# A two-way linear scan: own terms moved to identity and diagonal products in PSUM, and group statistics from an accumulator

## The chip, the cores and the metric

The kernel runs on one core of a Trainium2 chip. The metric is the device time of one execution in microseconds. Engines are named as in the profile: PE (matmuls), PEld (weight loads of the same engine), DVE (vector), ACT (scalar, activation functions), POOL and SP (here mostly the queue that issues DMAs).

## The reference

A network of four residual layers on `x` of shape 32 x 192 x 56 x 56 in fp32. Each layer normalises its input over 32 groups of 6 channels and adds its output to `x`. The layers are an agent attention (L0), a two-way RWKV scan (L1), a shift by learned offsets with a 3x3 filter (L2) and a long convolution with a 55x55 filter (L3). Only L1 is touched by the change. What matters of it (shortened, with the running maximum of the reference left out, which only guards against overflow):

```python
k, v, r = xs @ Wk.T, xs @ Wv.T, xs @ Wr.T          # xs: pixels x channels
def wkv(w, u, k, v):                               # per channel, along the pixels
    p = q = 0
    for t in pixels:
        y[t] = (p + exp(u + k[t]) * v[t]) / (q + exp(u + k[t]))
        p = exp(w) * p + exp(k[t]) * v[t]
        q = exp(w) * q + exp(k[t])
x_bi = 0.5 * (wkv(forwards) + wkv(backwards))
h = sigmoid(r) * x_bi
h = layernorm_over_channels(h) * ln_g + ln_b
x = x + h @ Wo.T
```

The term with `exp(u + k[t])` is called the own term here: a pixel's own contribution, weighted by `exp(u)`, that is added to what the recurrence carried up to the pixel before. The output `x` of this layer is called x2. The next layer needs its mean and variance per image and group of six channels.

## The kernel before, in words

The kernel has stages one after the other: the filter of L3 and the attention L0, then the scans of L1 (`scan_pairs`), then L2 and L3 together. `scan_pairs` works on pairs of images. A pair's 2 x 192 channels make three tiles of 128 partitions: the first 128 channels of either image, and the last 64 of both together. The 3136 pixels are cut into NM = 4 strips of MC = 784, and a matmul takes half a strip, 392 columns, since a PSUM bank holds 512 fp32 values. `turned()` hands out a PSUM tile of two banks, four of which rotate and fill PSUM. `_Pairs.outer` multiplies the first two tiles by a 192 x 192 weight, in parts called `aa` and `ca`, `_Pairs.inner` the third, in parts called `cc` and `ac`.

For one pair and strip there are four functions:

- `forwards` normalises x (ACT), multiplies by `wk` and `wv` (PE), takes `ek = exp(k)` (ACT) and `bv = ek * v` (DVE), and runs the forward scan.
- `backwards` multiplies the same normalised x by `wr`, makes the sigmoid `g` on ACT, and runs the backward scan over the stored `ek` and `bv`, from the last strip to the first. Then it forms `h = (y_f + y_b) * g` on DVE.
- `finish` centres `h` over the channels (`centre`, PE), squares it (ACT), averages the squares (`mean_w`, PE), multiplies `h` by `wog` (PE), scales by the inverse deviation (`rd`), adds the bias and x (L1170), takes `bn_stats` of the result for the next layer's group statistics (`stats_of`, L986), and stores x2.
- `measure` loads strips of a pair further on and takes `bn_stats` of them, for the first normalisation.

The main loop takes, for every pair and strip, `backwards` of this pair, `finish` of the strip before, `forwards` of the next pair, and in two of four steps two calls of `measure` for the pair after that. `deviations`, `norm` and `conclude` turn statistics into scales. `grouped` does small matmuls with one column for them. PE takes its instructions in the program's order. The order on DVE and ACT is made by a scheduler when the program is built.

The function `scan` is called once for each pair, strip, tile and direction. It handles two recurrences, `p` over `bv` and `q` over `ek`. DVE runs the recurrence with `tensor_tensor_scan` (L1070), writing it one column to the side, so that each pixel's place holds the state before it. POOL copies the carried state into the edge column and out of the last (L1065, L1071). Then DVE adds the own term by one `scalar_tensor_tensor` (L1072) on the whole strip:

```python
nc.vector.tensor_tensor_scan(out, decay[:, of(t)].to_broadcast([128, MC]), data, at, ALU.mult, ALU.add)
nc.gpsimd.tensor_copy(at, z[:, last : last + 1])
nc.vector.scalar_tensor_tensor(before, src, c, before, ALU.mult, ALU.add)
```

where `src` is `bv` or `ek` and `c` is `exp(u)`, one value per partition. `inverse` takes 1/q on ACT as a logarithm and an exponential (L1077, L1078), and DVE multiplies the two (L1113 forwards, L1134 backwards).

Of the kernel before, what the change touches and what calls it, by code (L numbers as in the profile page):

```python
# [876 lines left out]
def scan_pairs(ctx: ExitStack, tc: tile.TileContext, a, k, x1, x2, rs2, wogT, count):  # L877
# [15 lines left out]
    def small(name, shape):  # L893
        return cp.tile(shape, F32, name=name, tag=name)
# [6 lines left out]
        return [t[:, h * HM : (h + 1) * HM] for h in range(2)]  # L901


    wo = [small("wo_a", [128, C]), small("wo_c", [64, C])]
    lg = [small("lg_a", [128, 1]), small("lg_c", [64, 1])]
    lb = [small("lb_a", [128, 1]), small("lb_c", [64, 1])]
    cen = [small("cen_a", [128, C]), small("cen_c", [64, C])]
    for i, r in enumerate((slice(0, 128), slice(128, C))):
        nc.sync.dma_start(out=wo[i], in_=a["L1_conv_WoT"][r])
        nc.sync.dma_start(out=lg[i], in_=a["L1_conv_ln_g"][r].unsqueeze(1))  # L910
# [10 lines left out]
    for i, r in enumerate((slice(0, 128), slice(128, C))):  # L921
        n = (128, 64)[i]
        ps, _, _ = turned()
        for s in range(2):
            nc.tensor.matmul(ps[:n, 0, :C], cen[s][:, r], wo[s], start=(s == 0), stop=(s == 1))
        turn = wp.tile([128, C], F32, name="turn", tag="turn", bufs=1)
        nc.vector.tensor_copy(turn[:n], ps[:n, 0, :C])
        nc.sync.dma_start(out=wogT[r], in_=turn[:n])

    wk, wv, wr = (blocks(n, a[f"L1_conv_{n}T"]) for n in ("Wk", "Wv", "Wr"))  # L930
    wog, centre, mean_w, group = (
# [2 lines left out]
    wd = pairs.vector("wd", a["L1_conv_w_decay"])  # L934
    eu = pairs.vector("eu", a["L1_conv_u"])
    nc.scalar.activation(eu, eu, AF.Exp)

    w = small("w", [128, 2])
    nc.scalar.activation(w, wd, AF.Exp)
# [64 lines left out]
        pairs.inner(group, [ps[:, 1, 2:3]], [[s] for s in src])  # L1004
        return ps[:, :, 1], ps[:, 1, 2:3]

    def deviations(st):

        mv = moments(st)
        first, third = grouped([mv[:, t, 0:1] for t in range(3)])  # L1010
        mean = sp.tile([128, 3], F32, name="mean", tag="mean", bufs=4)
        nc.vector.tensor_copy(mean[:, 0:2], first)
        nc.vector.tensor_copy(mean[:, 2:3], third)
        d = sp.tile([128, 3], F32, name="d", tag="d", bufs=4)
        nc.vector.tensor_tensor(d, mv[:, :, 0], mean, ALU.subtract)
        nc.vector.tensor_tensor(d, d, d, ALU.mult)
        nc.vector.tensor_tensor(d, d, mv[:, :, 1], ALU.add)
        return mean, d
# [20 lines left out]
    class State:  # L1039


        def __init__(self, p, scaling):
            self.p, (_, self.rs, self.nb) = p, scaling
            self.seen = sp.tile([128, 5, 3 * NM], F32, name="seen", tag="seen", bufs=3)
            self.ek, self.bv, self.y = {}, {}, {}
            self.fore, self.back = start("f"), start("b")
            self.st2 = new_stats("st2")

    def normed(s, m):
        xs = load(s.p, m)  # L1050
# [1 line left out]
            nc.scalar.activation(xs[t], xs[t], AF.Identity, bias=s.nb[:, t : t + 1], scale=s.rs[:, t : t + 1])  # L1052
        return [parts(t) for t in xs]

    def scan(s, m, t, carry, rev):

        b, e = s.bv[m][t], s.ek[m][t]
        c = eu[:, of(t)]
        got = []
        for i, src in enumerate((b, e)):  # L1060
            z = wp.tile([128, MC + 1], F32, name="pq"[i], tag="pq", bufs=5)
            edge, last = (MC, 0) if rev else (0, MC)
            out, before = (z[:, 0:MC], z[:, 1:]) if rev else (z[:, 1:], z[:, 0:MC])
            at = carry[t][i]
            nc.gpsimd.tensor_copy(z[:, edge : edge + 1], at)  # L1065
            if rev:
                out, data = out[:, ::-1], src[:, ::-1]
            else:
                data = src[:, :]
            nc.vector.tensor_tensor_scan(out, decay[:, of(t)].to_broadcast([128, MC]), data, at, ALU.mult, ALU.add)  # L1070
            nc.gpsimd.tensor_copy(at, z[:, last : last + 1])  # L1071
            nc.vector.scalar_tensor_tensor(before, src, c, before, ALU.mult, ALU.add)  # L1072
            got.append(before)
        return got

    def inverse(s, den, m, t, which):
        nc.scalar.activation(den, den, AF.Ln)  # L1077
        nc.scalar.activation(den, den, AF.Exp, scale=-1.0, accum_out=s.seen[:, which, 3 * m + t : 3 * m + t + 1])  # L1078

    def start(way):  # L1080
        carry = [[sp.tile([128, 1], F32, name=f"{way}{i}{t}", tag=f"{way}{i}{t}") for i in range(2)] for t in range(3)]
# [5 lines left out]
    def forwards(s, m):  # L1087
        s.ek[m] = [kp.tile([128, MC], F32, name="ek", tag="ek") for _ in range(3)]
        s.bv[m] = [kp.tile([128, MC], F32, name="bv", tag="bv") for _ in range(3)]
        s.y[m] = [kp.tile([128, MC], F32, name="y", tag="y", bufs=3 * NM + 4) for _ in range(3)]  # L1090
        xn = normed(s, m)
        for tiles in ((0, 1), (2,)):
            for wt in (wk, wv):
                ps = [turned() for _ in tiles]
                if len(tiles) == 2:
                    pairs.outer(wt, [q[2] for q in ps], xn)
                else:
                    pairs.inner(wt, ps[0][2], xn)
                for t, (_, both, _) in zip(tiles, ps):
                    if wt is wk:  # L1100
                        nc.scalar.activation(
                            s.ek[m][t].rearrange("p (h n) -> p h n", h=2), both, AF.Exp,
                            accum_out=s.seen[:, 0, 3 * m + t : 3 * m + t + 1],
                        )
                    else:
                        nc.vector.tensor_tensor(
                            s.bv[m][t].rearrange("p (h n) -> p h n", h=2), both,
                            s.ek[m][t].rearrange("p (h n) -> p h n", h=2), ALU.mult,
                        )
            for t in tiles:  # L1110
                num, den = scan(s, m, t, s.fore, False)
                inverse(s, den, m, t, 1)
                nc.vector.tensor_tensor(s.y[m][t], num, den, ALU.mult)  # L1113

    def backwards(s, m):
        xn = normed(s, m)
        h = s.y[m]
        for tiles in ((0, 1), (2,)):
            ps = [turned() for _ in tiles]
            if len(tiles) == 2:  # L1120
                pairs.outer(wr, [q[2] for q in ps], xn)
            else:
                pairs.inner(wr, ps[0][2], xn)
            for t, (_, both, _) in zip(tiles, ps):
                g = wp.tile([128, MC], F32, name="g", tag="t")
                nc.scalar.activation(
                    g.rearrange("p (h n) -> p h n", h=2), both, AF.Exp, scale=-1.0,
                    accum_out=s.seen[:, 3, 3 * m + t : 3 * m + t + 1],
                )
                nc.scalar.activation(g, g, AF.Ln, bias=1.0)  # L1130
                nc.scalar.activation(g, g, AF.Exp, scale=-1.0)
                num, den = scan(s, m, t, s.back, True)
                inverse(s, den, m, t, 2)
                nc.vector.tensor_tensor(num, num, den, ALU.mult)  # L1134
                nc.vector.tensor_tensor(h[t], h[t], num, ALU.add)
                nc.vector.tensor_tensor(h[t], h[t], g, ALU.mult)

    def finish(s, m):
# [20 lines left out]
        for tiles in ((0, 1), (2,)):  # L1159
            po = [turned() for _ in tiles]  # L1160
            if len(tiles) == 2:
                pairs.outer(wog, [q[2] for q in po], hs)
            else:
                pairs.inner(wog, po[0][2], hs)
            for t, (_, out, _) in zip(tiles, po):
                rd = rds[t]
                rdh = rd.rearrange("p (h n) -> p h n", h=2)
                nc.scalar.activation(rd, rd, AF.Exp, scale=-0.5)
                nc.vector.tensor_tensor(rdh, out, rdh, ALU.mult)
                nc.vector.scalar_tensor_tensor(xs[t], rd, cb[:, of(t)], xs[t], ALU.add, ALU.add)  # L1170
                stats_of(s.st2, m, t, xs[t])
        rows = slice(m * MC // S, (m + 1) * MC // S)
        for r, t, i, c in places:
            nc.sync.dma_start(out=x2[c, i, rows, s.p], in_=xs[t][r].rearrange("p (h w) -> p h w", w=S))
# [20 lines left out]
        for t, x in enumerate(load(p, m)):  # L1195
            stats_of(st, m, t, x)

    s, after, before = State(0, norm(*deviations(stats_for(0)))), norm(*deviations(stats_for(1))), None
    for m in range(NM):
        forwards(s, m)  # L1200
    for p in range(last):
        ahead = State(p + 1, after) if p + 1 < last else None
        st = new_stats("st1")
        for i in range(NM):
            m = NM - 1 - i
            backwards(s, m)
            if i > 0:
                finish(s, m + 1)
            elif before is not None:
                finish(before, 0)  # L1210
            if ahead is not None:
                forwards(ahead, i)
            if p + 2 < last:
                if i < 2:
                    measure(st, p + 2, 2 * i)
                    measure(st, p + 2, 2 * i + 1)
                elif i == 2:
                    spread = deviations(st)
                else:
                    after = norm(*spread)  # L1220
            if before is not None:
                if i == 1:
                    before.spread = deviations(before.st2)
                elif i == 2:
                    conclude(before)
        before, s = s, ahead
    finish(before, 0)
    before.spread = deviations(before.st2)
    conclude(before)
    nc.sync.dma_start(out=rs2[0:128], in_=kept_a)  # L1230
    for i, r in enumerate((slice(0, 64), slice(64, 128))):
# [580 lines left out]
```

## Time and profile before

| | us |
|---|---|
| runs | 12775.48, 12757.16, 12770.67 |
| median | 12770.67 |
| profiled execution, its time | 12763.6 |
| profiled execution, its span | 12761.8 |

Of the span, the attention and all ahead of it take 0 to 4997 us, the set-up of the scans 4997 to 5081, the scans 5081 to 8816, the end of their statistics 8816 to 8830, and the two last layers the rest. The busy time of the engines over the span is PE 11522.3 us, PEld 7190.8, DVE 11221.3, ACT 5979.7 and POOL 2199.4.

The profile comes from one execution. Its slices show the busy share of each engine in tenths, PEclk the clock that was granted to PE. A row of a group gives the line, the engine, the operation, what it writes and reads, how often, then busy time in us and the mean of one in ns, and behind the last bar the idle time of that engine just before it, with what ended it. In the timeline the columns are start (us), duration (us), engine, line, operation and how many records are merged. An fp32 matmul of the code leaves two records on PE, and the records of following matmuls overlap.

### The profile page before, as it was taken

Reading aid. Unit: us, or ns where it says so; the run is one execution under the profiler, and the core shown is the slowest. Engines: PE = TensorE matmul, PEld = TensorE weight load, DVE = VectorE, ACT = ScalarE, POOL = GpSimd, SP = SyncE. Lnnn points to the kernel's source line nnn. Section 1 sums busy time; section 2 is a strip of 40 time slices with the busy share of each in tenths; the row PEclk is TensorE's granted clock in tenths of the full one; section 3 lists DMA queues with packets and bytes.
Section 4 is the critical chain, followed back from the end, with each engine's and each line's share of the span. In section 5 each row is a group of like instructions: output and inputs, shape, how many; then the busy total and the mean of one; then the engine's idle time right before and its main releaser. Section 6 shows DMA issues by size and latency. Waiting matters only on the chain. (4 is left out here: it accounts for less than half of the span.)

```text
span 12761.8 us, 165194 instructions
## 1 busy us (share of the span) xinstructions
PE 11522.3 (90%) x63158; PEld 7190.8 (56%) x63158; DVE 11221.3 (88%) x15929; ACT 5979.7 (47%) x11146; POOL 2199.4 (17%) x2238
## 2 busy tenths in 40 slices
PE   4999999999999997788878788787999999999999
PEld 1556555565555564333333333334777777777777
DVE  3888888888888886999999999998888888888888
ACT  2554554554554553555555555554333333333333
POOL 0000000000000000544445454544000000000000
PEclk8999999999999998889988899898999999999999
DMA  2111111111111112344443344433111111111111
GB/s 64 40 39 39 39 39 49 47 39 39 39 41 53 41 39 68 84 110 103 99 110 97 105 107 103 103 98 81 43 42 44 42 44 44 42 42 44 43 44 28
DMA packets 949574, 770.40 MB, mean 60 GB/s; under 512 B 769870, under 2 KB 811065, under 8 KB 939760
## 3 DMA queue, kind: packets, MB, share of 16 engines
q1 hardware_dynamic: 948776, 759.74, 22.7%
q8 instruction: 504, 8.26, 0.3%
q14 instruction: 294, 2.41, 0.1%
HBM read 479.96 MB, written 240.50 MB: 56 GB/s over the span
## 5 line engine op out<-in xcount | busy, mean ns | idle before, releaser
L589 DVE SCALAR_TENSOR_TENSOR o<-v_a,dww,o 128x896 f32<-128x896 f32 (+1 forms) x1024 | 1053.0, 1028 | 396.5 <-ACT v_a L563 314.2
L1739 ACT COPY y<-ps 64x252 f32<-64x252 f32 (+1 forms) x2376 | 806.4, 339 | 1132.6 <-PE ps L1733 1102.1
L1657 PE MATMUL ps<-f,real 84*84 84x112 f32 x6144 | 1090.8, 259 | 0.0
L1657 PE MATMUL ps<-f,imag 84*84 84x112 f32 x6144 | 1089.4, 259 | 0.0
L1664 ACT COPY z<-ps 84x448 f32<-84x448 f32 x768 | 405.0, 527 | 1219.9 <-PE ps L1657 1218.4
L1657 PEld LDWEIGHTS ps<-f,real 84*84 84x84 f32 x6144 | 783.9, 153 | 134.3 <-issue 95.8
L1084 POOL MEMSET f<- 128x1 f32 x96 | 8.8, 98 | 4810.6 <-PE ps L739 4805.6
L1077 ACT ACTIVATE q<-q 128x784 f32<-128x784 f32 x384 | 328.9, 857 | 999.1 <-DVE q L1072 753.0
L1657 PEld LDWEIGHTS ps<-f,imag 84*84 84x84 f32 x6144 | 763.8, 153 | 0.0
L606 ACT ACTIVATE pr<-ps,low 98x896 f32<-98x896 f32 (+1 forms) x384 | 351.9, 916 | 838.0 <-DVE low L604 838.0
L602 PE MATMUL ps<-xs_a,gk_a 128*98 128x448 f32 (+1 forms) x1536 | 637.8, 496 | 0.0
L589 DVE SCALAR_TENSOR_TENSOR o<-v_c,dww,o 128x448 f32<-128x448 f32 (+1 forms) x1024 | 634.1, 619 | 4.0
L603 PE MATMUL ps<-xs_c,gk_c 125*98 125x448 f32 (+1 forms) x1536 | 631.9, 492 | 0.0
L694 PE MATMUL ps<-gq_a,xs_a 128*112 128x294 f32 x1792 | 606.2, 419 | 19.2 <-DVE pq L699 19.2
L1674 PE MATMUL ps<-z,f 84*114 84x448 f32 x1536 | 608.9, 539 | 0.0
L695 PE MATMUL ps<-gq_c,xs_c 125*112 125x294 f32 x1792 | 596.4, 414 | 0.0
L1523 POOL TENSOR_TENSOR mat<-tap,tap 114x114 f32<-114x114 f32 x96 | 40.6, 423 | 3163.0 <-PE ps L1583 2310.0
L1631 PE MATMUL re<-y,f 128*84 128x420 f32 (+1 forms) x1152 | 532.0, 542 | 8.7 <-ACT y L1739 7.3
L1631 PE MATMUL im<-y,f 128*84 128x420 f32 (+1 forms) x1152 | 526.8, 538 | 0.0
L1733 PEld LDWEIGHTS ps<-f,padded 114*128 114x128 f32 x3168 | 471.5, 191 | 96.5 <-issue 70.4
L1733 PE MATMUL ps<-f,padded 114*128 114x168 f32 x3168 | 501.9, 310 | 21.4 <-DVE o L1676 10.0
L707 ACT ACTIVATE pq<-pq 112x1176 f32<-112x1176 f32 x224 | 265.3, 1184 | 525.1 <-DVE pq L699 401.9
(358 smaller groups left out, 29470.4 us busy)
## 6 DMA issues: line engine op xcount, KB each, us to landing
x<-x SPq DMA_DIRECT2D x640, 392.0 KB
x<-x SPq DMA_DIRECT2D x640, 196.0 KB
x<-x SPq DMA_DIRECT2D x192, 399.0 KB
out_x<-x SPq DMA_DIRECT2D x384, 196.0 KB
x_a<-in_x SPq DMA_DIRECT2D x32, 1568.0 KB
x<-x_a SPq DMA_DIRECT2D x32, 1568.0 KB
x_c<-in_x SPq DMA_DIRECT2D x64, 392.0 KB
x<-x_c SPq DMA_DIRECT2D x64, 392.0 KB
```

Of the source, the lines that this page charges most:

```text
L589: nc.vector.scalar_tensor_tensor(dst, tap(i), dww[:, t, i : i + 1], dst, ALU.mult, ALU.add)
L602: mm(ps[P2, h, :n], g[:, cols], xs_a[j][:, px], start=True, stop=False)
L603: mm(ps[P2, h, :n], gk_c[0:KC, 2 * j + h, cols], xs_c[j][0:KC, px], start=False, stop=True)
L606: nc.scalar.activation(pr[:, :, :n], ps[P2, :, :n], AF.Exp, bias=low[:, j, p : p + 1], accum_out=sums[:, j, p : p + 1])
L694: mm(ps[:SUB, i, :HA], xs_a[j][:, px], g, start=True, stop=False)
L695: mm(ps[:SUB, i, :HA], xs_c[j][0:KC, px], gq_c[0:KC, 2 * j + (q + i) // ns], start=False, stop=True)
L1631: nc.tensor.matmul(ps[:, : n * 84], f2[:, i, :], y[:, i0 : i0 + n].rearrange("p g s u -> p (g s u)"), start=True, stop=True)
L1657: nc.tensor.matmul(ps[:84, i * 2 * S : (i + 1) * 2 * S], part[:, i0 + i].rearrange("p s u -> p (s u)"), f3[:, m, :], start=(m == 0), stop= ...
L1664: nc.scalar.copy(z[:, i0 : i0 + n].rearrange("p g m w -> p (g m w)"), ps[:84, : n * 2 * S])
L1674: nc.tensor.matmul(got, f4[:, m, :], z[:, i0 : i0 + n, m, :], start=(m == 0), stop=(m == 1))
L1733: nc.tensor.matmul(ps[:, g * 168 : (g + 1) * 168], flat[:, (g0 + g) * 128 : (g0 + g + 1) * 128], f1, start=True, stop=True)
L1739: nc.scalar.copy(y[64 * m : 64 * m + 64, 2 * g0 + i : 2 * (g0 + n) : 2], got[64 * i : 64 * i + 64, :, :, m, :])
```

## The change

The own terms leave DVE. Two diagonal matrices `own[0]`, `own[1]` hold `exp(u)`, and `ident` is the identity, loaded by one more DMA at the set-up. For each recurrence of a scan, PE multiplies `src` by `own` and the shifted recurrence by `ident`, both into the same PSUM tile, for each half of the strip. The denominator `q` now goes first. ACT takes its logarithm from PSUM and writes the result into a tile of SBUF (`y` forwards, a new `den` backwards). The numerator stays in PSUM, where the final product on DVE reads it.

The statistics of x2 change too. The residual step (L1170 before) gives out the sum of its result by its accumulator. ACT squares the result about a near value, the negative mean of the last strip (which is the first that `finish` takes of a pair), and accumulates the squares. The two `bn_stats` per tile and strip of x2 are gone. `moments_of` makes mean and variance of the sums; the `bn_stats` of `measure` stay. A few constants of the set-up move into working tiles.

```diff
+    ident = small("ident", [128, 128])
+    nc.sync.dma_start(out=ident, in_=k["ident"])
+    own = [small(f"own{i}", [128, 128]) for i in range(2)]
+    for i in range(2):
+        nc.vector.tensor_scalar(own[i], ident, eu[:, i : i + 1], None, ALU.mult)
...
+    def moments_of(s):
+
+        mv = sp.tile([128, 3, 2], F32, name="mv2", tag="mv2")
+        nc.vector.tensor_reduce(mv[:, :, 0], s.sums, AX.X, ALU.add)
+        nc.vector.tensor_reduce(mv[:, :, 1], s.squares, AX.X, ALU.add)
+        nc.vector.tensor_scalar(mv, mv, 1.0 / N, None, ALU.mult)
+        nc.vector.tensor_tensor(s.away, s.away, mv[:, :, 0], ALU.add)
+        nc.vector.tensor_tensor(s.away, s.away, s.away, ALU.mult)
+        nc.vector.tensor_tensor(mv[:, :, 1], mv[:, :, 1], s.away, ALU.subtract)
+        nc.vector.tensor_scalar(mv[:, :, 1], mv[:, :, 1], 0.0, None, ALU.max)
+        return mv
...
-    def scan(s, m, t, carry, rev):
+    def scan(s, m, t, carry, rev, den, which):
 
-        b, e = s.bv[m][t], s.ek[m][t]
-        c = eu[:, of(t)]
-        got = []
-        for i, src in enumerate((b, e)):
+        for i, src in ((1, s.ek[m][t]), (0, s.bv[m][t])):
...
             nc.vector.tensor_tensor_scan(out, decay[:, of(t)].to_broadcast([128, MC]), data, at, ALU.mult, ALU.add)
             nc.gpsimd.tensor_copy(at, z[:, last : last + 1])
-            nc.vector.scalar_tensor_tensor(before, src, c, before, ALU.mult, ALU.add)
-            got.append(before)
-        return got
-
-    def inverse(s, den, m, t, which):
-        nc.scalar.activation(den, den, AF.Ln)
-        nc.scalar.activation(den, den, AF.Exp, scale=-1.0, accum_out=s.seen[:, which, 3 * m + t : 3 * m + t + 1])
+            _, both, halves = turned()
+            for w, rhs, first in ((own[of(t).start], src, True), (ident, before, False)):
+                for half, part in zip(halves, parts(rhs)):
+                    nc.tensor.matmul(half, w, part, start=first, stop=not first)
+            if i == 1:
+                nc.scalar.activation(den.rearrange("p (h n) -> p h n", h=2), both, AF.Ln)
+                nc.scalar.activation(
+                    den, den, AF.Exp, scale=-1.0, accum_out=s.seen[:, which, 3 * m + t : 3 * m + t + 1]
+                )
+        return both
...
             for t in tiles:
-                num, den = scan(s, m, t, s.fore, False)
-                inverse(s, den, m, t, 1)
-                nc.vector.tensor_tensor(s.y[m][t], num, den, ALU.mult)
+                y = s.y[m][t]
+                num = scan(s, m, t, s.fore, False, y, 1)
+                y = y.rearrange("p (h n) -> p h n", h=2)
+                nc.vector.tensor_tensor(y, num, y, ALU.mult)
...
-                num, den = scan(s, m, t, s.back, True)
-                inverse(s, den, m, t, 2)
-                nc.vector.tensor_tensor(num, num, den, ALU.mult)
-                nc.vector.tensor_tensor(h[t], h[t], num, ALU.add)
+                den = wp.tile([128, MC], F32, name="den", tag="t")
+                num = scan(s, m, t, s.back, True, den, 2)
+                both = den.rearrange("p (h n) -> p h n", h=2)
+                nc.vector.tensor_tensor(both, num, both, ALU.mult)
+                nc.vector.tensor_tensor(h[t], h[t], den, ALU.add)
...
-                nc.vector.scalar_tensor_tensor(xs[t], rd, cb[:, of(t)], xs[t], ALU.add, ALU.add)
-                stats_of(s.st2, m, t, xs[t])
+                nc.vector.scalar_tensor_tensor(
+                    xs[t], rd, cb[:, of(t)], xs[t], ALU.add, ALU.add, accum_out=s.sums[:, t, m : m + 1]
+                )
+                if m == NM - 1:
+                    nc.vector.tensor_scalar(
+                        s.away[:, t : t + 1], s.sums[:, t, m : m + 1], -1.0 / MC, None, ALU.mult
+                    )
+                nc.scalar.activation(
+                    rd, xs[t], AF.Square, bias=s.away[:, t : t + 1], accum_out=s.squares[:, t, m : m + 1]
+                )
```

More of the change, by code (lines that the diff above doesn't have):

```diff
@@ L901, in parts, with passing @@
         return [t[:, h * HM : (h + 1) * HM] for h in range(2)]
-    wo = [small("wo_a", [128, C]), small("wo_c", [64, C])]
+    def passing(n):
+        return wp.tile([128, MC], F32, name="passing", tag="t")[:n, :C]
+    wo = [passing(128), passing(64)]
     lg = [small("lg_a", [128, 1]), small("lg_c", [64, 1])]
     lb = [small("lb_a", [128, 1]), small("lb_c", [64, 1])]
-    cen = [small("cen_a", [128, C]), small("cen_c", [64, C])]
+    cen = [passing(128), passing(64)]
     for i, r in enumerate((slice(0, 128), slice(128, C))):
@@ L925, in scan_pairs @@
             nc.tensor.matmul(ps[:n, 0, :C], cen[s][:, r], wo[s], start=(s == 0), stop=(s == 1))
-        turn = wp.tile([128, C], F32, name="turn", tag="turn", bufs=1)
-        nc.vector.tensor_copy(turn[:n], ps[:n, 0, :C])
-        nc.sync.dma_start(out=wogT[r], in_=turn[:n])
+        turn = passing(n)
+        nc.vector.tensor_copy(turn, ps[:n, 0, :C])
+        nc.sync.dma_start(out=wogT[r], in_=turn)
     wk, wv, wr = (blocks(n, a[f"L1_conv_{n}T"]) for n in ("Wk", "Wv", "Wr"))
@@ L1005, in grouped, with deviations @@
         return ps[:, :, 1], ps[:, 1, 2:3]
-    def deviations(st):
-        mv = moments(st)
+    def moments_of(s):
[8 more added lines that the diff above has]
+        return mv
+    def deviations(mv):
         first, third = grouped([mv[:, t, 0:1] for t in range(3)])
@@ L1046, in __init__ @@
             self.fore, self.back = start("f"), start("b")
-            self.st2 = new_stats("st2")
+            self.sums, self.squares = (sp.tile([128, 3, NM], F32, name=n, tag=n, bufs=3) for n in ("sums", "squares"))
+            self.away = sp.tile([128, 3], F32, name="away", tag="away", bufs=3)
     def normed(s, m):
@@ L1196, in measure @@
             stats_of(st, m, t, x)
-    s, after, before = State(0, norm(*deviations(stats_for(0)))), norm(*deviations(stats_for(1))), None
+    s, after, before = State(0, norm(*deviations(moments(stats_for(0))))), norm(*deviations(moments(stats_for(1)))), None
     for m in range(NM):
@@ L1217, in scan_pairs @@
                 elif i == 2:
-                    spread = deviations(st)
+                    spread = deviations(moments(st))
                 else:
@@ L1222, in scan_pairs @@
                 if i == 1:
-                    before.spread = deviations(before.st2)
+                    before.spread = deviations(moments_of(before))
                 elif i == 2:
@@ L1227, in scan_pairs @@
     finish(before, 0)
-    before.spread = deviations(before.st2)
+    before.spread = deviations(moments_of(before))
     conclude(before)
```

## The prediction

> **What bounds the kernel now.** First the page's slices of the span, 319 us each.
>
> ```profile
> PE   4999999999999997788878788787999999999999
> PEld 1556555565555564333333333334777777777777
> DVE  3888888888888886999999999998888888888888
> ACT  2554554554554553555555555554333333333333
> ...
> PEclk8999999999999998889988899898999999999999
> ```
>
> Slices 16 to 27 are the scan stage, the only one whose code changes. There DVE is at 9 and PE, elsewhere at 9, is at 7 or 8 with a lower granted clock. So DVE is full and PE has gaps. How large the gaps are is the question, and next comes the table by stretches. The scan stage runs from the first `Wk` matmul (5081) to the last `wog` matmul (8816). The second row is a stretch of the later stages, where PE is the full engine.
>
> ```profile
> core 0: us, PE busy (x) PEld busy (x) DVE busy (x) ACT busy (x) POOL busy (x), PEclk, DMA share, GB/s
> 5081.00:8816.00 3735.00, 3031.46 (x10800) 1385.79 (x10802) 3656.97 (x4059) 2163.80 (x3578) 1862.21 (x1699) 0.90 0.40 101
> 9100.00:12700.00 3600.00, 3557.20 (x24277) 2742.15 (x24276) 3119.30 (x5241) 1289.90 (x3109) 262.84 (x395) 1.00 0.17 42
> ```
>
> DVE is busy for 3657 of 3735 us (98%): it sets this stage. PE is busy for 3031 us at a mean clock of 0.90. Without gaps it had 1.00, so its work at full clock is about 3031 x 0.90 = 2728 us, and 3735 - 2728 = 1007 us is what PE could still take. Next, the groups of that stretch on DVE, for what goes away.
>
> ```profile
> L1072 DVE SCALAR_TENSOR_TENSOR q<-ek,eu,q 128x784 f32<-128x784 f32 x384 | 391.8, 1024 | 0.5
> L1072 DVE SCALAR_TENSOR_TENSOR p<-bv,eu,p 128x784 f32<-128x784 f32 x384 | 386.5, 1020 | 0.0
> L986 DVE BATCH_NORM_STATS2 st<-x 128x6 f32<-128x392 f32 x714 | 361.6, 554 | 6.2 <-DMA x<-x 6.2
> ```
>
> Last, PE's timeline where it runs without gaps at full clock, for the price of what is added.
>
> ```profile
> 6553.32 1.58 PE L870 MATMUL ps<-x,Wk_cc 128*128 128x392 f32 x4
> 6554.84 1.54 PE L873 MATMUL ps<-x,Wk_ac 128*64 128x392 f32 x8
> 6556.30 1.58 PE L870 MATMUL ps<-x,Wv_cc 128*128 128x392 f32 x4
> 6557.82 1.54 PE L873 MATMUL ps<-x,Wv_ac 128*64 128x392 f32 x8
> 6559.28 0.38 PE L1002 MATMUL ps<-d,grp_aa 128*128 128x1 f32 x2
> ...
> 6561.05 2.90 PE L860 MATMUL ps<-x,Wr_aa 128*128 128x392 f32 x8
> ...
> 6570.37 2.90 PE L860 MATMUL ps<-y,cen_aa 128*128 128x392 f32 x8
> 6573.20 1.59 PE L863 MATMUL ps<-y,cen_ca 64*128 64x392 f32 x8
> 6574.72 1.58 PE L870 MATMUL ps<-y,cen_cc 128*128 128x392 f32 x4
> 6576.23 1.54 PE L873 MATMUL ps<-y,cen_ac 128*64 128x392 f32 x8
> ```
>
> The column to read is the start, not the duration: matmuls overlap in the records, so a group costs the distance to the next group's start. Each matmul of the code leaves two records (both `cc` matmuls of a group are "x4"). Two full 128x128 matmuls on 392 columns with one weight (`cc`) cost 1.51 to 1.52 us, four (`aa`) 2.83, four half-height ones (`ca`) 1.52, four half-width ones (`ac`) 1.46. So a further record costs about 0.33 us ((2.83 - 1.515) / 4), and a change of weight about 0.2 us on top (1.515 - 4 x 0.33).
>
> **The sum for PE.** There are 16 pairs x 4 strips = 64 steps. A step has five weights at 2.83 + 1.52 + 1.51 + 1.46 = 7.32 us (`wk`, `wv`, `wr`, `centre`, `wog`) and `mean` at 2.83 + 1.52 = 4.35: 40.95 us, 2621 us for 64. The small group sums (58 at 6561.05 - 6559.28 = 1.77 us) add 103: 2724 us, which agrees with the 2728 above. The change adds, per scan, `own` on `ek`, `ident` on `q`, `own` on `bv`, `ident` on `p`, two full matmuls each: four `cc`-like groups of 1.515 us, 6.06 us. With 64 x 3 tiles x 2 directions = 384 scans that is 384 x 6.06 = 2327 us. PE then has 2724 + 2327 = 5051 us to do in a stage that takes 3735. It has 1007 us of room and gets 2327.
>
> The Trainium skill, "TensorE: Matmul & The Clock Gate", section "Back-to-back issue gap", gives N/2.4 + 2.5 ns for a warm matmul, 166 ns for 392 columns; by that the addition would be an estimated 510 us and fit. The rows above say 0.66 us for the two records, and they decide. The skill's "Perfetto Trace Analysis", section "Identifying the Most-Contended Engine", would judge TensorE's headroom by weight loads rather than matmul time; by PEld's 1386 of 3735 us (37%) PE would be far from full here, and DVE's saving would be the gain. The start-to-start distances contradict that for 392-column fp32 matmuls.
>
> **DVE.** Removed: 768 multiply-adds (L1072) at 1.02 us by the rows, 786 us, and the 384 `bn_stats` of x2 (L986) at 0.55, 213 us. Records of DVE overlap a little, so the gain is nearer 900 than 999 us. Added: seven small operations instead of three `bn_aggr` per pair, 48 copies of -sum/784, `own`: a few us. The accumulator on the residual step (L1170) is not in the trace on DVE; ScalarE's read of its accumulator takes 0.19 us, so 0 to 0.19 x 192 = 36 us. The final products now read PSUM; L1169, which does so, takes 0.96 us like L1113, which does not: nothing. DVE falls to about 2770 us.
>
> **ACT.** 192 squares like L1149's (0.81 + 0.19 us) add 193 us, and the logarithm of the denominators reads PSUM (L1126's 0.81 instead of L1077's 0.86), -18. ACT goes from 2164 to about 2340 us, far from full. POOL's 128x1 copies stay; the products on `ident` now wait for the one that fills the edge column, as L1077 did.
>
> **What becomes late.** PE runs in the program's order, while DVE's order is a scheduled one: in the changed kernel as built DVE does both tiles' scans (`q`, `q`, `bv`, `bv`, `p`, `p`) before the first final product. So while PE spends 6.06 us on a scan's products, DVE needs 2 x 1.84 + 0.96 = 4.6 us for it, and the next `ident` finds its scan done. What can stop PE is a strip of `x`. In two of four steps the strips that are measured for a later pair share the seven `x` buffers, and their `bn_stats` stand on DVE ahead of the `rd` products that free PSUM for `wk` and `wv`. Before, PE lost 176 + 80 us waiting for a normalised `x` (L860, L863 on ACT L1052) by the waits of PE, the nearest rows there are. The bounds are 0 and 256; I take 150, since the DVE queue that made some of these waits is now short. The set-up's one more DMA and two small products are a few us at most.
>
> Stage: 5051 + 150 = 5201 us, against 3735: +1466. The profiled execution took 12763.6 us, so 14230; the median of the runs is 7 us above it, so 14237, say **14240 us**. The cover for DVE's saving is gone the other way round: DVE's 900 us fall into time in which PE is the last to finish.
>
> **Rivals.**
> *Cheaper changes of weight.* If the load of `ident` or `own` hides behind the running matmuls, 1536 groups lose 0.2 us, 307 us: 13930. Against it, every `cc` row shows the gap, with 128-column weights of the same size.
> *PE waits for each scan.* If DVE held a tile's scan behind the previous tile's final product, `ident` would come 0.96 + 1.84 - 1.515 = 1.3 us late, 384 times: 499 us, 14740. DVE's scheduled order speaks against it, PE's fixed order and four PSUM tiles for it.
> *Not slower.* The new products cost one record each, not two, or overlap in pairs as `ca` does. Break-even is (3735 - 2724) / 3072 = 0.33 us per matmul, one record. Below it DVE's 2770 us and PE share the stage; at half of that PE has 2724 + 507 + 150 = 3381 and the time is about 12410. Against it: these are full 128x128 fp32 matmuls like `cc`, which never shows under 0.66.
> *The change half works.* If the squares or the PSUM readers held up ACT, the time would still be PE's, as ACT has 2860 us to spare.
>
> **How the numbers follow.** Forecast 0.80; cheaper weights 0.07; waiting for scans 0.10; not slower 0.03, of which most is faster. The range goes from 13960, near the cheaper weights, to 14560, which takes the whole 256 us of strip waits and part of the wait for scans. A difference of 0.2% (25 us) is what the runs can tell from none: faster 0.02, same 0.01, slower 0.97.
>
> **What would show it.** After: PE near 97% busy through the stage at a granted clock of 1.00, DVE near 53%, `own` and `ident` groups 1.51 us apart, PE the stage's chain. The lines of L1072 and half of L986 are gone. It is wrong if DVE is still at 95% or more, if the new groups stand well under 1.3 us apart, or if PE shows idle time in front of `ident`, released by scans, of more than 300 us in sum.

## The result, and the profile after

| | before | after |
|---|---|---|
| median of the runs, us | 12771.16 (12757.16 to 12775.48) | 13877.79 (13871.16 to 13887.6) |
| profiled execution, time and span | 12763.6, 12761.8 | 13871.16, 13869.4 |
| scan stage, first `Wk` to last `wog` | 5081 to 8816: 3735 | 5069.7 to 9920.7: 4851 |
| DVE busy in the stage | 3657 | 2895 |
| PE busy in the stage, granted clock | 3031 at 0.90 | 4794 at 0.99 |

The change makes the kernel slower: the ratio is 1.0869, with an interval of 1.085 to 1.0888. The forecast said 14240 with a range from 13960. The direction and the engine were right, and the time fell below the range.

The slices of the page after, now 347 us each; slices 14 to 28 are the scan stage.

```profile
PE   4999999999999979999999999999899999999999
PEld 2656556556556545555555555555577777777777
DVE  4888888888888866565656656565588888888888
ACT  2455455554554534545454544545433333333333
...
PEclk8999999999999989999999999999999999999999
```

PE and DVE have changed places. Between the two end slices, which also hold other stages, PE is at 9 with its full clock, and DVE is at 5 or 6. The table by stretches gives the numbers.

```profile
core 0: us, PE busy (x) PEld busy (x) DVE busy (x) ACT busy (x) POOL busy (x), PEclk, DMA share, GB/s
5069.70:9920.70 4851.00, 4793.75 (x16942) 2457.73 (x16940) 2894.52 (x3211) 2419.67 (x3956) 669.74 (x1699) 0.99 0.32 78
```

PE is busy for 99% of the stage and DVE for 60%. On DVE the multiply-adds of the own terms are gone; of `bn_stats` the strips of `measure` are left, and the accumulator is read 190 times at 0.081 us (groups of the stage on DVE):

```profile
L995 DVE BATCH_NORM_STATS2 st<-x 128x6 f32<-128x392 f32 x336 | 176.4, 560 | 369.4 <-DMA x<-x 368.6
L1194 DVE DVE_READ_ACCUMULATOR x<-rd,cb,x 128x1 f32 x190 | 15.4, 81 | 0.0
```

What counts is the price of the new groups. This is PE's timeline from the forward scans of tiles 0 and 1 to the third tile. Again the column to read is the start.

```profile
7048.38 1.59 PE L863 MATMUL ps<-x,Wv_ca 64*128 64x392 f32 x8
7049.90 1.58 PE L1094 MATMUL ps<-ek,own 128*128 128x392 f32 x4
7051.32 1.48 PE L1094 MATMUL ps<-q,ident 128*128 128x392 f32 x4
7053.09 1.55 PE L1094 MATMUL ps<-bv,own 128*128 128x392 f32 x4 [0.29 <-DVE bv L1128]
7055.73 1.56 PE L1094 MATMUL ps<-p,ident 128*128 128x392 f32 x4 [1.08 <-DVE p L1089]
7057.12 1.48 PE L1094 MATMUL ps<-ek,own 128*128 128x392 f32 x4
7058.44 1.48 PE L1094 MATMUL ps<-q,ident 128*128 128x392 f32 x4
7059.75 1.48 PE L1094 MATMUL ps<-bv,own 128*128 128x392 f32 x4
7061.07 1.48 PE L1094 MATMUL ps<-p,ident 128*128 128x392 f32 x4
7062.39 1.48 PE L870 MATMUL ps<-x,Wk_cc 128*128 128x392 f32 x4
7063.80 1.54 PE L873 MATMUL ps<-x,Wk_ac 128*64 128x392 f32 x8
7065.27 1.58 PE L870 MATMUL ps<-x,Wv_cc 128*128 128x392 f32 x4
7066.78 1.54 PE L873 MATMUL ps<-x,Wv_ac 128*64 128x392 f32 x8
7068.25 1.59 PE L1094 MATMUL ps<-ek,own 128*128 128x392 f32 x4
```

From 7057.12 to 7062.39 four groups, each with another weight than the one before, stand 1.317 us apart. That is four records of 0.329 us and nothing for the change of weight. The same `cc` form costs 1.41 us where a full group stands ahead and a half-width one behind (`Wk_cc`, 7062.39 to 7063.80), and 1.51 where half-width groups stand on both sides (`Wv_cc`, 7065.27 to 7066.78). So what the forecast took for a change of weight goes with the change of *form*: about 0.1 us in a full group's distance at each border to half tiles. In the kernel before, a full group had half tiles ahead of it, behind it or on both sides; of the 1536 new groups 256 have such a border and the others none.

The waits of PE in the stage:

```profile
PE ps L1094 <- DVE p L1089: 31.3, 29, 1.1
PE ps L1094 <- DVE bv L1128: 23.9, 27, 1.1
```

These are waits for the first tile's numerator in some of the steps, as at 7053 and 7055 above. The waits for a strip of `x` that the forecast had put at 150 us are gone.

### The profile page after: what moved, and what is told of

It reads as the page before. It is cut to its first block, busy times and chain, and to the rows that moved or that the text cites. A ratio compares the mean times of both kernels' runs of the same rounds, so it can differ in the third digit from the quotient of the medians.

```text
span 13869.4 us, 177711 instructions
## 1 busy us (share of the span) xinstructions
PE 13277.6 (96%) x69302; PEld 8267.0 (60%) x69302; DVE 10454.9 (75%) x15083; ACT 6239.0 (45%) x11530; POOL 1006.9 (7%) x2238
## 5 line engine op out<-in xcount | busy, mean ns | idle before, releaser
L1094 PE MATMUL ps<-p,ident 128*128 128x392 f32 x1536 | 571.0, 494 | 31.3 <-DVE p L1089 31.3
L1094 PE MATMUL ps<-ek,own 128*128 128x392 f32 x1536 | 594.9, 510 | 0.2 <-ACT ek L1123 0.2
L1094 PE MATMUL ps<-bv,own 128*128 128x392 f32 x1536 | 570.0, 494 | 23.9 <-DVE bv L1128 23.9
L1089 DVE TENSOR_TENSOR_SCAN p<-decay,b,bv 128x784 f32<-128x784 f32 x192 | 353.8, 1843 | 316.3 <-PE ps L1094 310.1
L1094 PE MATMUL ps<-q,ident 128*128 128x392 f32 x1536 | 569.5, 493 | 1.5 <-DVE q L1089 1.3
L1074 ACT ACTIVATE x<-x,nb,rs 128x784 f32<-128x784 f32 x384 | 396.1, 1033 | 318.2 <-DMA x<-x 196.4
```

The lines of the kernel that those rows point to most:

```text
L1094: nc.tensor.matmul(half, w, part, start=first, stop=not first)
```

## The experiments

The medians of the kernel before in these runs were 12762.1 us (e1 to e4), 12768.72 (e5 to e8) and 12769.82 (e9 to e12).

### What a change of weight costs (e1)

Matmuls alone on data at rest, in sections, with everything else taken out. It computes nothing of the reference and ran once. Three of its sections (shortened, `mm` is the matmul):

```python
    # 2 two weights in turn, on top
    for i in range(G):
        for h in range(2):
            mm(p[i // 2 % 2][h], (wa, wb)[i % 2], (s, o)[i % 2][h], start=i % 2 == 0, stop=i % 2 == 1)
    # 3 two weights in turn, each product another weight
    for i in range(2 * G):
        mm(p[0][0] if i % 2 else p[1][0], (wa, wb)[i % 2], s[0], start=True, stop=True)
...
    # 5 full, then four of half width in another tile of PSUM
    for i in range(G // 2):
        for h in range(2):
            mm(p[i % 2][h], wa, s[h], start=True, stop=True)
        for h in range(2):
            for r in (low, high):
                mm(p[2 + i % 2][h][r], wn, o[h], start=True, stop=True)
```

> A kernel of matmuls alone (it computes nothing of the reference; the output is x with four numbers of the products in it). All products are fp32 on 392 columns, in seven stretches behind one of warming up: one full 128x128 weight; the same, each pair on top of the pair before in PSUM; two full weights in turn, pair by pair; two in turn, product by product; a full pair and four half-width products on top of it, as cc and ac; the same with the half-width products in another PSUM tile; four full and four half-height ones, as aa and ca; half-width ones alone. Theory (what costs is the change between full and half tiles, about 0.1 us or a little more each way; a change of weight between full tiles is hidden): full pairs 1.32 us apart in all stretches with full tiles alone, also when the weight changes with every product (0.66 us each); full pair plus half-width four 2.98 us, whether on top or in another PSUM tile; four full plus four half-height 4.35 us; half-width fours alone 1.32. Rival of the prediction (a change of weight costs 0.2 us): pairs with two weights in turn 1.515, product by product 0.86. Second rival (adding on top of what was just written costs): 1.32 for one weight on fresh tiles, more for one weight on top, and 2.63 for the half-width products in another tile.

Its timeline, one stretch from each of three sections:

```profile
134.11 1.48 PE L49 MATMUL p<-src,wa 128*128 128x392 f32 x4
135.43 1.48 PE L49 MATMUL p<-other,wb 128*128 128x392 f32 x4
...
258.54 0.82 PE L52 MATMUL p<-src,wb 128*128 128x392 f32 x2
259.20 0.82 PE L52 MATMUL p<-src,wa 128*128 128x392 f32 x2
...
334.95 1.58 PE L63 MATMUL p<-src,wa 128*128 128x392 f32 x4
336.46 1.54 PE L66 MATMUL p<-other,wn 128*64 128x392 f32 x8
```

Two weights in turn stand 1.32 us apart, as one weight does, and product by product 0.66. A full pair takes 1.51 us next to groups of half width, and the pair and the four after it 2.98 together, though they write PSUM tiles of their own. Full groups alone take 1.317 and half-width groups alone 1.314, so two borders cost 2.98 - 2.63 = 0.35, or 0.17 each, 0.1 of it in the full group's distance. So neither the change of weight nor adding on top of a product in PSUM has a price; the border between forms does.

One thing limits this. PEld shows a weight load for every record, also where the weight stays the same: 189 loads for 190 records in the section with one weight, 191 for 192 where each product has another. The table of the kernel before shows it too (10802 loads, 10800 records). So a change saves or costs no load here; what a weight would save that is loaded once and kept, no run shows.

The Trainium skill ("TensorE: Matmul & The Clock Gate", section "Back-to-back issue gap") would give a warm matmul on 392 columns an estimated 166 ns (N/2.4 + 2.5). Here a full fp32 one takes 0.66 us, in two records of 0.33, and in no run is it shorter.

### The border of forms inside the changed kernel (e9)

Against after: for the third forward tile both full products first, then both half-width ones.

```diff
+            if len(tiles) == 1:
+                both = [[turned()] for _ in range(2)]
+                for wt, q in zip((wk, wv), both):
+                    for h, o in enumerate(q[0][2]):
+                        nc.tensor.matmul(o, wt[3], xn[2][h], start=True, stop=False)
+                for wt, q in zip((wk, wv), both):
+                    for h, o in enumerate(q[0][2]):
+                        for t, r in enumerate((slice(0, 64), slice(64, 128))):
+                            nc.tensor.matmul(o[r], wt[2], xn[t][h], start=False, stop=True)
...
-                    pairs.inner(wt, ps[0][2], xn)
+                    ps = both[0 if wt is wk else 1]
```

> The changed kernel with one order altered on PE: for the third tile of forwards, both cc groups (wk, wv) come first and both ac groups behind them, in place of cc, ac, cc, ac. The number of weights loaded is the same; there are two changes fewer between full and half tiles per step. Theory (the change of tile form costs, not the change of weight): in the trace the four groups go from 1.41 + 1.47 + 1.515 + 1.47 = 5.86 us to about 5.5 us, 64 x 0.35 = 22 us in all, 13855 us. Rival (each change of weight costs 0.2 us): 5.86 us as before, 13878 us.

Measured: 13901.75 us (13894.36 to 13912.62), 24 us slower than after, where 22 us faster was the theory. Its timeline:

```profile
7001.79 1.48 PE L1119 MATMUL ps<-x,Wk_cc 128*128 128x392 f32 x4
7003.10 1.48 PE L1119 MATMUL ps<-x,Wv_cc 128*128 128x392 f32 x4
7004.52 1.54 PE L1123 MATMUL ps<-x,Wk_ac 128*64 128x392 f32 x8
7005.88 1.49 PE L1123 MATMUL ps<-x,Wv_ac 128*64 128x392 f32 x8
7007.30 1.58 PE L1094 MATMUL ps<-ek,own 128*128 128x392 f32 x4
7009.05 1.55 PE L1094 MATMUL ps<-q,ident 128*128 128x392 f32 x4 [0.16 <-DVE q L1089]
```

The four groups take 5.51 us in place of 5.86 (7062.39 to 7068.25 in after). That is 0.35 us for two borders fewer, as in e1, and 22 us in the sum over the stage. But `k` of the third tile now ends a group later, so `ek` and the scan of `q` do too, and the next `ident` stands 1.75 us behind its `own` in place of 1.42. The waits of PE have the new line, 76 times where after had 5:

```profile
PE ps L1094 <- DVE q L1089: 14.5, 76, 0.4
```

The distances from `own` to `ident` grew by 28 us in the sum and those from `ident` to `own` by 10, the stage by 15 (4866). The other 9 us lie ahead of the stage, whose code is the same; in the profiled executions of all kernels the stage began between 5070 and 5092 us, and I have no cause for that.

### The two halves of the change (e2, e3, e5)

e2 keeps `bn_stats` for x2 and has the rest of the change, the products with their order and `den`; e3 has the statistics, the new order (`q` first) and the tile `den`, with the own terms on DVE; e5 is the kernel before with the statistics alone.

```diff
 # e3, against after
-            _, both, halves = turned()
-            for w, rhs, first in ((own[of(t).start], src, True), (ident, before, False)):
...
+            nc.vector.scalar_tensor_tensor(before, src, eu[:, of(t)], before, ALU.mult, ALU.add)
+            both = before.rearrange("p (h n) -> p h n", h=2)
```

> The products in PSUM as changed, but x2's statistics by bn_stats as before. Theory (PE alone sets the stage): DVE gets 384 x 0.47 = 180 us back and has over 1900 us to spare, so the time is that of the changed kernel, 13880 us within 0.3%. Rival (half of the change is worth its own DVE time whatever PE does): 14060 us.

> The own terms on DVE as before, x2's statistics by the accumulator and the squares as changed. Theory (DVE sets the stage of the kernel before): 384 bn_stats, 0.47 us apart, leave it, 180 us, and the accumulator gives back 0 to 36 us: 12590 to 12630 us. Rival (ACT's three squares in front of the exponentials of the next strip make DVE wait, or DVE pays for the accumulator): 12770 us or more.

> The kernel before with the statistics half alone, and nothing of the scans' new order or of the new den tile (the earlier run of this half had both). Theory (the half itself costs DVE nothing and saves its bn_stats; the earlier run lost by the den tile and the order of q and p): 12590 to 12640 us. Rival (ACT's squares in front of the next strip's exponentials hold up DVE): 12770 us or more, near the earlier 13017.

e2 took 13942.49 us (13939.75 to 13950.82), e3 13016.58 (12997.22 to 13028.03), e5 12714.38 (12707.09 to 12725.5). The loss comes with the products: with the statistics left as they were it is 1.0927 (1.0909 to 1.0945). e2 is 65 us over after, more than was expected. Its stage is 4897 us, 46 over after's, and begins 21 later. DVE has 164 us more to do there, and PE waits longer for it: the distances on PE from `ident` to `own` grew by 23 us, those from `own` to `ident` by 10, and those at `Wv_aa`, which waits for `rd`, by 18.

e5 is the fastest kernel here, at 0.9957 (0.994 to 0.9974). Its expectation was 12590 to 12640. DVE's busy time in the stage fell by 156 us (3657 to 3501) but the stage by only 51 (3735 to 3684), since DVE now waits for ACT:

```profile
DVE q L1083 <- ACT ek L1114: 75.8, 46, 8.8
DVE p L1147 <- ACT q L1091: 67.9, 60, 2.8
```

Before, the two same waits were 8.8 and 37.1 us:

```profile
DVE p L1134 <- ACT q L1078: 37.1, 42, 1.5
DVE q L1070 <- ACT ek L1101: 8.8, 1, 8.8
```

e3 was expected at 12590 to 12630 and missed that by nearly 400 us, the next thing to find.

### The tile `den` (e6, e10)

e3 and the whole change put the backward denominators into `den` under the tag `t`, whose eight buffers `sq`, `rd` and `g` also use. e6 does that alone on the kernel before; e10 gives `den` a buffer of its own. Both move a few constants of the set-up into working tiles for room.

```diff
-                num, den = scan(s, m, t, s.back, True)
-                inverse(s, den, m, t, 2)
-                nc.vector.tensor_tensor(num, num, den, ALU.mult)
-                nc.vector.tensor_tensor(h[t], h[t], num, ALU.add)
+                num, q = scan(s, m, t, s.back, True)
+                den = wp.tile([128, MC], F32, name="den", tag="t")             # e6
+                den = wp.tile([128, MC], F32, name="den", tag="den", bufs=1)   # e10
+                nc.scalar.activation(den, q, AF.Ln)
...
+                nc.vector.tensor_tensor(den, num, den, ALU.mult)
+                nc.vector.tensor_tensor(h[t], h[t], den, ALU.add)
```

> The kernel before, with the backward scans' inverse written to a den tile of the working buffers (tag t) in place of q itself, as the change does; no products, no new statistics. Theory (twelve tiles a step from eight buffers, in place of nine, make sq and rd wait for the backward scans' last products, and DVE waits for what follows): 12900 to 13000 us. Rival (the buffers are enough): 12770 us.

> The kernel with the den tile alone (13204 us), but den in one buffer of its own, so that g, sq and rd again share eight buffers with nine tiles a step. Theory (the 436 us came from sq and rd waiting for buffers that the late products of the backward scans held): most of it goes, 12770 to 12900 us; one buffer for three tiles may cost some. Rival (the added tile made ACT or the scheduled order worse in itself): 13100 us or more.

e6 took 13204.52 us (13198.49 to 13211.08), 436 more than before, e10 12774.68 (12763.38 to 12791.6), no different from before (1.0008, 0.9998 to 1.0018). The same wait of PE in both, e6 first:

```profile
PE ps L860 <- ACT sq L1154: 698.0, 63, 13.5
```

```profile
PE ps L860 <- ACT sq L1154: 229.9, 62, 8.7
```

With a buffer of its own for `den`, the loss goes and PE's wait for the squares of `finish` falls to a third. So it is the sharing of the tag `t` that costs, 436 us where DVE sets the stage. This is more than e3 lost: e3 is 254 us over before, with the 54 us that the statistics save in it. What made `den` cheaper there, the order with `q` first for one, was not tested by itself. In after, where PE sets the stage, PE's waits list none for `sq`, and `den` costs nothing that PE's waits show.

### Moving less (e4, e7, e8, e11, e12)

At 1.317 us a group, PE's room of 1007 us holds half of the own terms: 64 x 12 x 1.317 = 1011. So it could pay to move only the denominators. e4 does so within the changed kernel, e7 for the forward scans only, on the kernel before; e8 is e7 with the statistics; e11 and e12 are e7 and e8 without the third tile.

```diff
 # e4, against after: products for the denominators alone
+            if i == 1:
+                _, both, halves = turned()
...
+            else:
+                nc.vector.scalar_tensor_tensor(before, src, eu[:, of(t)], before, ALU.mult, ALU.add)
+                both = before.rearrange("p (h n) -> p h n", h=2)
 # e7 (e11), against before
-            nc.vector.scalar_tensor_tensor(before, src, c, before, ALU.mult, ALU.add)
+            if i == 1 and not rev and (True):     # e11: (t < 2)
+                _, both, halves = turned()
...
+                before = both
+            else:
+                nc.vector.scalar_tensor_tensor(before, src, c, before, ALU.mult, ALU.add)
```

> As changed, but only the denominators q go through PE; the numerators' own terms stay on DVE, so 1536 products instead of 3072. PE sets the stage by either price, DVE has about 3120 us. Theory (own and ident at 1.32 us a pair, 0.1 us more where a half tile stands next): 2724 + 384 x 2.7 = 3760 us of PE, the stage 3800 with 1% of slow clock, 12840 us. By the price of the prediction (1.515 us): 2724 + 1163 = 3890, 12960 us. Rival (the two engines, almost level, wait for each other): over 13000 us.

> The kernel before, with the products in PSUM for the denominators of the forward scans alone, which need no den tile (y takes the logarithm): 768 products on PE, 192 own terms off DVE. By the rows DVE has 3657 - 192 x 0.935 = 3477 us and PE 2724 + 192 x 2.7 = 3243. Theory (the busier engine sets the stage, here still DVE): 12770 - 180 = 12590 us, some more where the two wait for each other. Rival (any product between two scans costs a round trip from DVE to PE and ACT): 12770 or more.

> The last two halves together: forward denominators on PE, x2's statistics by accumulator and squares. DVE 3657 - 180 - 180 = 3300 us, PE 3243: the split at which the engines are level. Theory: 12770 - 360 = 12410 us, up to 12500 with waits between level engines. Rival (level engines in fixed orders wait for each other, as with half the products): 12700 or more.

> The kernel before, with products in PSUM for the forward denominators of the first two tiles alone; the third tile's own term stays on DVE, since there PE waited 3.6 to 5 us for the scan, with everything of the next strip queued behind. DVE 3657 - 128 x 0.935 = 3537 us, PE 2724 + 128 x 2.7 = 3070. Theory (a product costs only where PE, in its fixed order, waits for a scan): 12770 - 120 = 12650 us, to 12750. Rival (the products cost by PE's time in the cycle of a strip, waits or not): 12770 or more.

> The same with x2's statistics by accumulator and squares, which alone gave 12714 us. Theory (the two gains add): 12590 to 12680 us, the fastest of all. Rival (as above): 12714 or more.

| | median, us | ratio (interval) |
|---|---|---|
| e4, all denominators | 13196.08 | 1.0337 (1.0319 to 1.0354) |
| e7, forward denominators | 12951.01 | 1.0147 (1.013 to 1.0164) |
| e8, e7 and statistics | 12887.39 | 1.0095 (1.0078 to 1.0111) |
| e11, tiles 0 and 1 of e7 | 12793.02 | 1.0018 (1.0008 to 1.0027) |
| e12, e11 and statistics | 12744.19 | 0.9983 (0.9973 to 0.9993) |

The theory that the smaller move wins fell each time; e12 is a little faster than before, but slower than the statistics alone (e5). The first waits of PE in the stage, for e4, e7 and e11 in this order:

```profile
PE ps L1095 <- DVE q L1089: 257.6, 65, 6.3
```

```profile
PE ps L1085 <- DVE q L1079: 234.9, 52, 7.6
```

```profile
PE ps L860 <- ACT sq L1171: 281.2, 78, 6.1
```

In e4 PE was busy 3922 us at a clock of 0.95 in a stage of 4181. 3922 x 0.95 = 3726 us of work is close to 2724 + 1011 = 3735, so the price holds. PE stands idle for 259 us, 258 of them in front of an `ident` for its scan, and the other 196 us are what the lower clock costs, by the same product. PE takes its program in order, so with that `ident` the next step's work waits too. DVE's longest wait in e4, 321 us for PE's product ahead of `rd`, fits this, but it was not tested by itself. e11 takes out the third tile, whose scan comes soonest after its `k`, and with it nearly all of e7's loss. In e11 DVE's busy time in the stage is 3558 us, 100 less than before, but DVE's wait for ACT at `rd` is 129 us where before had 15, and PE's wait for `sq` 281 where before had 163. So DVE's saving comes back as waits for ACT:

```profile
DVE rd L1191 <- ACT rd L1190: 128.5, 44, 6.7
```

That is as far as these runs go; an order of the program made for the smaller move was not tried.

## Why the prediction was wrong in size and right in kind

*Which engine.* Right. PE is busy for 99% of the stage at a clock of 0.99, as the forecast (97%, 1.00) had it. The Trainium skill's "Identifying the Most-Contended Engine" ("Perfetto Trace Analysis") would judge the headroom of PE by its share of peak FLOPs and by its weight loads. PEld stands at 2458 of 4851 us, 51%, in a stage that PE fills, so the weight loads do not show it; the share of peak FLOPs was not worked out here.

*The price of a group: the step that failed.* It reads "a change of weight about 0.2 us on top (1.515 - 4 x 0.33)". 0.33 per record was right; the 0.2 is not the change of weight but two borders between full and half tiles. By it the change should have added 384 x 6.06 = 2327 us; at 1.317 it is 1536 x 1.317 = 2023, 304 less. Every `cc` row that it quotes stands between two `ac` or `ca` rows, so these could not price a full group among full groups. By them the cost lay between 1.32 and 1.515, and both ends belonged in the range. The kernel before had a row that tells the two readings apart, 30 us further on in the same timeline:

```profile
6584.13 5.81 PE L860 MATMUL ps<-sq,mean_aa 128*128 128x392 f32 x8 [6.36 <-ACT sq L1149]
6589.78 0.82 PE L860 MATMUL ps<-y,wog_aa 128*128 128x392 f32 x2
6590.53 1.59 PE L863 MATMUL ps<-sq,mean_ca 64*128 64x392 f32 x8
```

One product of `wog_aa` stands behind `mean_aa`, full tiles with another weight, and ahead of half-height ones. It takes 0.75 us: 0.66 for its two records and 0.09 for the border behind it. A change of weight at 0.2 would have made it 0.86. (In the code `wog` comes behind all of `mean`, so PE's order, too, is that of the program as built and not always that of the code.) The forecast gave the low end, the first rival at 13930, a chance of 0.07, and the range ended above it at 13960. With 1.32 and none of the 150 us of waits it would have reached down to 13780.

*The rivals.* "Cheaper changes of weight" came true: its 13930 is 52 us above the result. PE did not wait for each scan: it stood idle for 57 us in front of the new groups, not 499. And the products do cost two records each, so "not slower" failed where the forecast said.

*The waits.* 150 us was taken for strips of `x`; those waits vanished (0.3 us at L860, and that for `rd`). By the distances on PE, the new groups take 74 us more than 1.317 us each and the borders explain. These are lost ahead of `own` and `ident`, nearly all at the first forward tile, whose `bv` and `p` DVE has not ready. Another 24 us are in twelve `Wr_aa` groups that run long (below). Together 98, 52 less than the 150, and from other causes: that the term came this near is luck.

*DVE.* The durations of its records sum to 3981 us before and 3031 after, 949 less, between the forecast's 900 and 999. Its busy time fell by only 762, to 2895 and not 2770, since its records overlapped by 323 us when it was full and by 136 now. PE, the fuller engine, hides this. ACT was busy for 2420 us, 80 more than forecast; PE waited for it once, for 0.2 us.

*The sum.* The forecast stage was 5201 us. Less 304 for the groups and 52 for the waits it is 4845; measured 4851. The 6 us more fit the borders that came and went: 256 `own` groups have half tiles ahead and take 1.42 us, 27 us in all, while `cen_aa`, `Wk_cc` and `Wr_cc` lost a border and take 0.10 us less, 20 us in all. The stage began 12 us earlier and what follows took 3 more: 14230 - 304 - 52 + 6 - 12 + 3 = 13871, the profiled execution.

## What to carry to other kernels

Price an added instruction from a row whose neighbours have the form that the new one's neighbours will have; where no such row exists, both ends of the price belong in the range. When work moves to the engine that has room, check in program order what stands behind each new wait: here even the part that fitted into PE's room by the sum lost its gain to an `ident` that came before its scan. Try the parts of a change by themselves: the statistics alone gave 0.4% that the whole change buried.

## What the hardware showed unexpectedly

- Changing the weight between full 128x128 fp32 tiles on 392 columns is free (1.317 us a pair with one or two weights, 0.66 product by product), while a border between full and half-width tiles costs about 0.17 us, in e1 and in e9 against after. Between full and half-height tiles it is about 0.2 us, estimated from e1: four full products and four half-height ones take 4.35 us together, 0.40 more than their records at 0.33 us each (half-height ones, in pairs, stand 0.33 apart within their group). Half-height tiles alone were not run.
- In twelve of the 64 steps `Wr_aa` took 4.3 to 5.5 us to the next start and not 2.83, with no wait listed. All twelve stand behind an unbroken run of one-column matmuls of 3.4 to 4.1 us. Behind 32 shorter runs (1.7 to 1.8 us) and one of 3.4 us `Wr_aa` took 2.83. In one of the twelve, shown here, the granted clock was 0.64 from 6617 to 6625 and 1.00 from 6625 to 6700. So the long runs and the lower clock go together; no run here changed them, so that they cause it is not shown.

```profile
6617.54 0.38 PE L873 MATMUL ps<-d,grp_ac 128*64 128x1 f32 x4
6617.85 5.34 PE L860 MATMUL ps<-x,Wr_aa 128*128 128x392 f32 x8
```

- Reading DVE's accumulator took 0.081 us in after (L1194), where reading ACT's took 0.19 in before (L1149).
- POOL's busy time in the stage fell from 1862 to 670 us with the same 1699 instructions: the groups of its 128x1 copies had means of 0.63 to 1.71 us before and of 0.18 to 1.18 after. DVE was full in the one and not in the other; that this is the cause was not tested.
